# Layer 0's queries on four 64x64 quarters of TensorE, with a second copy of x by columns

## The chip, the core and the metric

The kernel runs on one core of one Trainium2 chip. A core has five engines that follow their own queues and meet by semaphores: TensorE (PE; its weight loads are listed apart as PEld), VectorE (DVE), ScalarE (ACT), GpSimd (POOL), and SyncE (SP), which here only issues DMAs. Matmuls write to PSUM, eight banks of 2 KB in each of 128 partitions. [...]The metric is the device time of one execution in microseconds.

## What is computed

Two graph layers over 16 batches of 1024 nodes with 64 features; `adj` is a 1024x1024 adjacency matrix for each batch, with some eight neighbours for a node and the node itself.

```python
# layer 0: eight heads of 64
q = (x @ Wq + bq);  k = (x @ Wk + bk);  v = (x @ Wv + bv)       # split in heads
s = leaky_relu(q k^T / 8 + edge_bias[adj], 0.2)                 # -1e9 where adj == 0
x = layernorm(x + (softmax(s) v) @ Wp + bp)
# layer 1: additive attention, one head
hp = x @ lin_w^T + lin_b;  u = hp W1^T;  v = hp W2^T
e = leaky_relu(u_i + v_j, 0.2) . a                              # masked by adj
x = layernorm(x + elu(softmax(e) hp))
```

Since few neighbours are set, the kernel builds a list of neighbours for every group of eight nodes and works on gathered columns alone. The weights of queries and keys are multiplied into one 64x64 matrix for each head beforehand (`aqk`), so that the scores of a node are its transformed x against its neighbours' plain x.

## The kernel before

**Tiles and steps.** A batch is eight tiles of 128 nodes. `xs` holds x with a row of the batch on each partition: partitions 0 to 63 have nodes of the first half of the batch (0 to 511), 64 to 127 of the second. Tile t is then 64 nodes of either half. `columns_T` turns it by matmuls against the identity into `xT`: partition d holds feature d of the first half, partition 64 + d feature d of the second, and columns `ts(t, 64)` are tile t's 64 nodes of each half.

One loop over steps g = 0, 1, ... does one tile of layer 0 and one of layer 1, which lags by 12 tiles, in a software pipeline whose order is written out by hand: a step gathers tile g, computes its queries, scores tile g-1, finishes tile g-2, and so on. Each engine gets its instructions in the order in which the program names them, so a queue's order is that of the loop's body. In the part that matters here a step issues:

1. `exps` and `score` of the tiles before (`s` L616, `sc` L624, `ls`, `mx`),
2. `gather` of layer 0's tile, both halves (`pg` L504, copied by ScalarE to `xg`, L510), with `heads` (`po` L684) between,
3. `rows` of layer 1 and, in odd steps, of layer 0 (`back`, L280 and L700),
4. `queries` (`pq` L599 on TensorE, `qp` L600 on VectorE),
5. the residuals (`o` L815, `y` L706 and the moments) and `den` L649 on VectorE,
6. layer 1's `project` (`pz` L750 and L756 on TensorE, Relu L761 on ScalarE, `r` L762 on VectorE),
7. layer 1's first gather half, its `turn_weights` (L790, copied as `eT` by VectorE, L792) and layer 0's `turn` (`pt` L523, copied as `xn` by ScalarE, L524),
8. `weigh` (`e` L776), which takes `r` and needs the bank that `eT` has read, the second gather half, `turn_weights` of layer 0 (`pp` L658, copied as `w`, L660), `attend` (`z` L668 and `pa` L801).

At five places of a step (`lists.place`) VectorE gets a share of the work that builds the next batch's neighbour lists; how much is due at each place is a fixed plan (`QUOTA`). At the end of step t == 4 of a batch, the next batch's `Layer0` is made: its constructor calls `begin`, which transposes x (`px` L274) and has ScalarE copy it to `xT` (L532). `score` of the next step is the next TensorE work.

**Banks.** PSUM's eight banks are shared by pools: `ps_g` (two banks: gathers, `pq`, `px`, layer 1's turn, `pa`), `ps_s` (two: scores, `pz`, `po`), `ps_p` (two: layer 0's turn `pt` and its turned weights `pp`), and `ps_z` (one each for two tags). A tile takes the bank that was used two tiles earlier in its pool and waits until that one's last reader is done.

**The queries.** For every head h and half n a matmul has 128 rows: `aqk[:, n, h, :]` holds the head's matrix on the 64 partitions of half n and zeros on the other 64, so the 128 rows of `xT` give half n alone. The outputs of the halves go to partitions `sub(n)`, 0 to 63 or 64 to 127, of one bank. A weight of 128 rows by 64 columns is shown as 128*64 in the profile; an fp32 matmul that is no transpose has two records.

Other parts of the kernel use all four quarters of TensorE, two blocks of 64 rows by two of 64 columns. They go through them in the order of `CORNERS`, with one bank for each row block:

```python
CORNERS = ((0, 0), (1, 1), (0, 1), (1, 0))      # (row block n, column block c_)
for n, c_ in CORNERS:                           # project, L756
    nc.tensor.matmul(pz[n][sub(c_), p, :], ub[sub(n), 2 * p + c_, :], rw[sub(n), :], start=False, stop=(p == 3))
```

`constants` (`prc` L585), `score` L616, `heads` L684 and `project` do so.

Of the kernel before, what the change touches and what calls it, by code (L numbers as in the profile page):

```python
# [9 lines left out]
F32 = mybir.dt.float32  # L10
I32 = mybir.dt.int32
AF = mybir.ActivationFunctionType
ALU = mybir.AluOpType
# [9 lines left out]
GR = 8  # L23
# [10 lines left out]
def kernel(  # L34
# [4 lines left out]
    nc = tc.nc  # L39
    B, N, D = x.shape  # L40
    H = edge_bias.shape[1]
    HD = H * D
    P = 128
# [9 lines left out]
    fst = fast.enter_context(tc.tile_pool(name="fst", bufs=1))  # L53
# [3 lines left out]
    ident = cst.tile([P, P], F32, name="ident")  # L57
# [7 lines left out]
    def sub(n):  # L65
        return slice(n * D, n * D + D)
# [6 lines left out]
    def bank(name):  # L73
        return ps_c.tile([P, 4, P], F32, tag="c", name=f"ps_{name}")

    def halves(name, cols_):

        t = fst.tile([P] + cols_, F32, tag=name, name=name)
        nc.gpsimd.memset(t, 0.0)
        return t  # L80
# [19 lines left out]

    bq_c, bk_c, bv_c = (columns(b, n) for b, n in ((bq, "bq_c"), (bk, "bk_c"), (bv, "bv_c")))
    QS1 = 1.0 / float(D) ** 0.5
    aqk = halves("aqk", [2, H, D])
    wvp = fst.tile([P, H, D], F32, name="wvp")
    qb = fst.tile([P, H], F32, name="qb")
    wc8 = halves("wc8", [GR, H, GR])
    wc1 = tmp.tile([1, H], F32, name="wc1")
    for h in range(H):
        c, r = h // 2, sub(h % 2)
        pw = bank(f"h_{h}")  # L110
        pc = bank(f"hc_{h}")
        for n in range(2):
            o = sub(n)
            nc.tensor.matmul(pw[o, 0, 0:D], wqT[r, c, :], wkT[r, c, :], start=True, stop=True)
            nc.tensor.matmul(pw[o, 1, 0:D], wvT[r, c, :], wp_l[r, c, :], start=True, stop=True)
            nc.tensor.matmul(pw[o, 2, 0:1], wkT[r, c, :], bq_c[r, c : c + 1], start=True, stop=True)
            nc.tensor.matmul(pw[o, 3, 0:1], wqT[r, c, :], bk_c[r, c : c + 1], start=True, stop=True)
            nc.vector.tensor_scalar(aqk[o, n, h, :], pw[o, 0, 0:D], QS1, None, ALU.mult)
            nc.vector.tensor_copy(wvp[o, h, :], pw[o, 1, 0:D])
            for i in range(GR):  # L120
                nc.vector.tensor_scalar(wc8[o, i, h, i : i + 1], pw[o, 3, 0:1], QS1, None, ALU.mult)
        nc.vector.tensor_scalar(qb[:, h : h + 1], pw[:, 2, 0:1], QS1, None, ALU.mult)
        nc.tensor.matmul(pc[0:1, 0, 0:1], bq_c[r, c : c + 1], bk_c[r, c : c + 1], start=True, stop=True)
        nc.vector.tensor_scalar(wc1[:, h : h + 1], pc[0:1, 0, 0:1], QS1, None, ALU.mult)
# [7 lines left out]
    pw = bank("wcb")  # L132
# [7 lines left out]
    pw = bank("bpv")  # L140
# [15 lines left out]
    pw = bank("ww")  # L156
# [7 lines left out]
    pw = bank("lin")  # L164
    for n in range(2):
        o = sub(n)
# [7 lines left out]
    pw = bank("ub")  # L174
# [5 lines left out]
    pw = bank("rows_b")  # L180
    nc.tensor.matmul(pw[:, 0, 0 : 2 * D], ones[0:1, :], ub_r.rearrange("o k d -> o (k d)"), start=True, stop=True)
    nc.vector.tensor_copy(rows_b.rearrange("p k d -> p (k d)"), pw[:, 0, 0 : 2 * D])
    NQ = D // GR
# [63 lines left out]
    CORNERS = ((0, 0), (1, 1), (0, 1), (1, 0))  # L247
# [12 lines left out]
    dbl = fast.enter_context(tc.tile_pool(name="g_dbl", bufs=2))  # L260
    sml = fast.enter_context(tc.tile_pool(name="g_sml", bufs=4))
    ps_g = fast.enter_context(tc.tile_pool(name="ps_g", bufs=2, space=bass.MemoryType.PSUM))
    ps_s = fast.enter_context(tc.tile_pool(name="ps_s0", bufs=2, space=bass.MemoryType.PSUM))
    ps_p = fast.enter_context(tc.tile_pool(name="ps_p", bufs=2, space=bass.MemoryType.PSUM))
# [2 lines left out]
    def by_rows(ap, n):  # L267
        return ap[n * 512 : n * 512 + 512, :].rearrange("(t r) d -> r t d", r=D)

    def columns_T(ps, src):  # L270

        for t in range(NT):
            for n in range(2):
                nc.tensor.matmul(ps[sub(n), ts(t, D)], src[:, t, :], ident[:, sub(n)], start=True, stop=True)  # L274

    def rows_T(ps, src, w):

# [184 lines left out]
    class Tiles:  # L462
# [63 lines left out]
        def begin(self, x_):  # L526

            b = self.b
            px = ps_g.tile([P, 512], F32, tag="g", name=f"px{self.layer}_{b}")
            columns_T(px, x_)  # L530
            self.xT = dbl.tile([P, 512], F32, tag=f"xT{self.layer}", bufs=2 - self.layer, name=f"xT{self.layer}_{b}")
            nc.scalar.copy(self.xT, px)  # L532
            self.t3, parts = thirds(x_, "x3", f"{self.layer}_{b}")
            self.f, self.xg, self.xn = {}, {}, {}
            lists.side.insert(0, parts)
# [5 lines left out]
    class Norm:  # L541


        def __init__(self, nm):
            self.nm = nm
            self.mv = sml.tile([P, NT, 2], F32, tag="mv", name=f"mv_{nm}")
# [20 lines left out]
    class Layer0(Tiles):  # L567
        layer = 0

        def __init__(self, b):  # L570
            self.b, self.cb, self.xs = b, {}, inputs[b]
            self.begin(self.xs)
            self.mx = dbl.tile([P, 2, NG // 4], F32, tag="mx", name=f"mx_{b}")
            self.y = dbl.tile([P, NT, D], F32, tag="y", bufs=3, name=f"y0_{b}")
            self.norm = Norm(f"0_{b}")
            self.qp, self.ls, self.den, self.w = {}, {}, {}, {}
# [16 lines left out]
        def queries(self, t):  # L593
            nm = f"{self.b}_{t}"
            qp = dbl.tile([P, NQ, H, GR], F32, tag="qp", name=f"qp_{nm}")
            pq = ps_g.tile([P, H, D], F32, tag="g", name=f"pq_{nm}")
            for h in range(H):
                for n in range(2):
                    nc.tensor.matmul(pq[sub(n), h, :], aqk[:, n, h, :], self.xT[:, ts(t, D)], start=True, stop=True)  # L599
            nc.vector.tensor_tensor(  # L600
                qp.rearrange("p q h i -> p h q i"), pq.rearrange("p h (q i) -> p h q i", i=GR),
                qb.unsqueeze(2).unsqueeze(3).to_broadcast([P, H, NQ, GR]), ALU.add,
            )
            self.qp[t] = qp

        def score(self, t, between):
# [274 lines left out]
    with tc.manual_schedule(engines={getattr(mybir.EngineType, e) for e in order}):  # L881
# [12 lines left out]
        for g in range(NT * B + LAG + 7):  # L894
            u = g - LAG
            b, t = divmod(g, NT)
# [472 lines left out]
```

## Time and profile before

| | |
|---|---|
| median of 3 runs | 2506.59 us (2506.02 to 2509.31) |
| the profiled execution | 2508.34 us, its span 2506.5 us |
| PE, PEld busy | 2296.7 us (92%), 1951.9 us (78%) |
| DVE, ACT, POOL busy | 1930.4, 1450.3, 1010.8 us |
| `pq` L599 | 4096 records, 222 ns each, 141.9 us busy |
| `qp` L600 | 128 instructions, 689 ns each, 88.2 us busy |
| `px` L274 of layer 0 | 512 records, 20.0 us busy |
| `xT` copy L532 | 32 instructions, 585 ns each |

Records of TensorE overlap, so 222 ns is the latency of one, not its share of the time; what a block costs is read from the starts in the timeline or from the chain. An engine's busy share is a mean over the span. The first 95 us are setup and the first batch's lists, the steps with queries run to 2344 us, and the rest is layer 1 alone.

### The profile page before, as it was taken

Reading aid. Unit: us, or ns where it says so; the run is one execution under the profiler, and the core shown is the slowest. Engines: PE = TensorE matmul, PEld = TensorE weight load, DVE = VectorE, ACT = ScalarE, POOL = GpSimd, SP = SyncE. Lnnn points to the kernel's source line nnn. Section 1 sums busy time; section 2 is a strip of 40 time slices with the busy share of each in tenths; the row PEclk is TensorE's granted clock in tenths of the full one; section 3 lists DMA queues with packets and bytes.
Section 4 is the critical chain, followed back from the end, with each engine's and each line's share of the span. In section 5 each row is a group of like instructions: output and inputs, shape, how many; then the busy total and the mean of one; then the engine's idle time right before and its main releaser. Section 6 shows DMA issues by size and latency. Waiting matters only on the chain.

```text
span 2506.5 us, 111153 instructions
## 1 busy us (share of the span) xinstructions
PE 2296.7 (92%) x48706; PEld 1951.9 (78%) x48706; DVE 1930.4 (77%) x5237; ACT 1450.3 (58%) x4401; POOL 1010.8 (40%) x1490
## 2 busy tenths in 40 slices
PE   5377999999999999999999999999999999999996
PEld 3266778888887888878888887878888887888864
DVE  6586868888887888888788878878787887866543
ACT  0054565666565665656566665656566665666743
POOL 1033433535344353534445353444534444443431
PEclk9988999999999999999999999999999999999998
DMA  3313242333224233323324232332423233231211
GB/s 102 109 43 117 81 143 77 104 116 109 91 81 138 77 117 103 121 77 100 120 77 140 81 119 77 113 107 78 142 86 113 83 111 103 66 96 61 69 38 29
DMA packets 192705, 239.03 MB, mean 95 GB/s; under 512 B 91732, under 2 KB 157332, under 8 KB 192212
## 3 DMA queue, kind: packets, MB, share of 16 engines
q1 hardware_dynamic: 192212, 231.85, 30.3%
q8 instruction: 384, 6.29, 1.0%
q14 instruction: 109, 0.89, 0.1%
HBM read 226.58 MB, written 5.21 MB: 92 GB/s over the span
## 4 chain that ended last, share of the span: by engine, by line
PE 66%; DVE 25%; DMA 3%; ACT 2%; issue 2%; POOL 1%; SPq 0%; POOLq 0%; ACTq 0%; DVEq 0%
PE pg L504 21%; PE s L616 5%; PE pt L523 5%; PE z L668 5%; DVE r L762 4%; PE pz L750 4%; PE pp L658 4%; PE pa L801 4%; PE pq L599 4%; PE pz L756 4%; PE po L684 3%; PE e L776 3%; DVE f L480 3%; DMA ad<-in_adj_dram 2%; PE pat L334 2%
## 5 line engine op out<-in xcount | busy, mean ns | idle before, releaser
L504 PE MATMUL pg<-f,x 128*64 128x272 bf16 (+2 forms) x13312 | 806.1, 273 | 40.4 <-DVE f L480 34.6
L504 PEld LDWEIGHTS <-x 128*64 128x64 bf16 x13312 | 662.8, 109 | 119.2 <-issue 73.8
L650 POOL TENSOR_TENSOR ls<-ls,den 128x480 f32<-128x480 f32 x256 | 298.5, 1166 | 579.8 <-DVE den L649 577.0
L510 ACT COPY xg<-pg 128x448 f32<-128x448 f32 x512 | 271.8, 531 | 392.4 <-PE pg L504 392.2
L480 DVE TENSOR_SCALAR f<-cb,jrow 128x2176 bf16<-128x2176 bf16 x512 | 409.0, 843 | 1.2 <-DMA cb<-col_d 1.0
L642 ACT ACTIVATE ls<-ls,mx 128x120 f32<-128x120 f32 x1024 | 391.2, 386 | 0.0
L524 ACT COPY xn<-pt 120x512 f32<-120x512 f32 x512 | 277.9, 598 | 22.7 <-PE pt L523 21.0
L523 PE MATMUL pt<-ident,xg 128*120 128x128 f32 x2048 | 269.6, 274 | 0.4
L761 ACT ACTIVATE r<-pz 128x480 f32<-128x480 f32 x256 | 132.2, 568 | 220.3 <-PE pz L756 220.3
L523 PEld LDWEIGHTS pt<-ident,xg 128*120 128x120 f32 x2048 | 229.4, 138 | 7.3 <-ACT xg L510 2.8
L489 POOL COPY xg<-xT 128x64 f32<-128x64 f32 x256 | 98.8, 396 | 307.1 <-PE pt L523 307.1
L762 DVE SCALAR_TENSOR_TENSOR r<-pz,r 128x480 f32<-128x480 f32 x256 | 155.9, 651 | 74.9 <-ACT r L761 74.6
L624 DVE TENSOR_TENSOR sc<-s,rowc 128x480 f32<-128x480 f32 x256 | 155.5, 649 | 71.2 <-PE s L616 69.3
L642 ACT ACTIVATION_READ_ACCUMULATOR ls<-ls,mx 128x1 f32 x1024 | 194.5, 190 | 0.0
L558 POOL TENSOR_TENSOR rs<-mv,eps 128x2 f32<-128x2 f32 x128 | 32.3, 253 | 379.0 <-DVE den L649 299.4
L632 DVE SCALAR_TENSOR_TENSOR ls<-sc 128x480 f32<-128x480 f32 x256 | 175.7, 686 | 0.0
L633 DVE TENSOR_REDUCE mx<-ls 128x4 f32<-128x480 f32 x256 | 167.2, 653 | 8.8
L756 PEld LDWEIGHTS pz<-rw,ub 64*64 64x64 f32 x4096 | 118.8, 133 | 63.2 <-issue 62.2
L600 DVE TENSOR_TENSOR qp<-pq,qb 128x512 f32<-128x512 f32 x128 | 88.2, 689 | 102.2 <-PE pq L599 101.0
L668 PE MATMUL z<-w,xn 120*64 120x64 f32 x4096 | 160.2, 229 | 4.8 <-ACT w L660 4.0
L658 PE MATMUL pp<-ident,ls 128*120 128x128 f32 x1024 | 143.0, 281 | 22.9 <-POOL ls L650 16.0
L668 PEld LDWEIGHTS z<-w,xn 120*64 120x64 f32 x4096 | 139.0, 141 | 28.6 <-ACT w L660 26.0
(212 smaller groups left out, 4092.7 us busy)
## 6 DMA issues: line engine op xcount, KB each, us to landing
cb<-col_d SPq DMA_DIRECT2D x271, 544.0 KB
ad<-in_adj_dram SPq DMA_DIRECT2D x256, 256.0 KB
xs<-in_x_dram SPq DMA_DIRECT2D x32, 128.0 KB
rows_s<-slot_d SPq DMA_DIRECT2D x256, 14.0 KB
out_dram<-o SPq DMA_DIRECT2D x32, 128.0 KB
col_d<-col SPq DMA_DIRECT2D x128, 4.2 KB
dg<-in_adj_dram SPq DMA_DIRECT2D x32, 2.0 KB
slot_d<-slot SPq DMA_DIRECT2D x16, 28.0 KB
```

The costliest lines, as they stand in the source:

```text
L480: nc.vector.tensor_scalar(fj.rearrange("p s n q k -> p (s n q k)"), cb.rearrange("p s n q k -> p (s n q k)"), jrow[:, j : j + 1], None, AL ...
L504: nc.tensor.matmul(pg[sub(n), :, FIRST * a_ + lo : FIRST * a_ + to], self.t3[:, k, 4 * hs + 2 * a_ + j, :], f[j][:, 2 * hs + a_, n, :, lo:to],
L510: nc.scalar.copy(dst, pg)
L523: nc.tensor.transpose(pt[:, q, :], xg[:, 4 * m + q, :], ident)
L524: nc.scalar.copy(self.xn[t][:, ts(m, 4), :], pt)
L632: nc.vector.scalar_tensor_tensor(ls, scs[n], SLOPE, scs[n], ALU.mult, ALU.max)
L642: nc.scalar.activation(ls[:, q, :], ls[:, q, :], AF.Exp, bias=neg[:, q : q + 1], accum_out=den[:, q : q + 1])
L650: nc.gpsimd.tensor_tensor(ls, ls, den.unsqueeze(2).to_broadcast([P, 4, SLOTS]), ALU.mult)
L658: nc.tensor.transpose(pt[:, p, :], ls[:, p, :], ident)
L668: nc.tensor.matmul(zz[sub(n), q, :], xn[:, q, sub(n)], w_[n][:, q // 2, sub(q % 2)], start=True, stop=True)
L756: nc.tensor.matmul(pz[n][sub(c_), p, :], ub[sub(n), 2 * p + c_, :], rw[sub(n), :], start=False, stop=(p == 3))
L762: nc.vector.scalar_tensor_tensor(r, pz[n], SLOPE / (1.0 - SLOPE), r, ALU.mult, ALU.add)
```

## The change

Before, `aqk` had for each half its own copy with zeros; now it is stored once on partitions 0 to 63 and once on 64 to 127, with no zeros, and a matmul uses 64 rows. Row block n computes heads 4n to 4n + 3, for both halves of the nodes. Row block 0 finds the first half of x in `xT`, but needs the second half on partitions 0 to 63 too, and row block 1 the first half on 64 to 127. So the constructor makes a second transpose `xo` with the halves exchanged (`columns_T` with `other=1`), again through a bank of `ps_g` and a ScalarE copy. The number of query matmuls stays 16 for a tile. Their outputs go to two banks, one for each row block, taken from `ps_p` and not from `ps_g`, and VectorE adds `qb` in two instructions of 256 columns, not one of 512.

```diff
-    aqk = halves("aqk", [2, H, D])
+    aqk = fst.tile([P, H, D], F32, name="aqk")
...
-            nc.vector.tensor_scalar(aqk[o, n, h, :], pw[o, 0, 0:D], QS1, None, ALU.mult)
+            nc.vector.tensor_scalar(aqk[o, h, :], pw[o, 0, 0:D], QS1, None, ALU.mult)
...
-    def columns_T(ps, src):
+    def columns_T(ps, src, other=0):
         for t in range(NT):
             for n in range(2):
-                nc.tensor.matmul(ps[sub(n), ts(t, D)], src[:, t, :], ident[:, sub(n)], start=True, stop=True)
+                nc.tensor.matmul(ps[sub(n), ts(t, D)], src[:, t, :], ident[:, sub(n ^ other)], start=True, stop=True)
...
             self.begin(self.xs)
+            px = ps_g.tile([P, 512], F32, tag="g", name=f"pxo_{b}")
+            columns_T(px, self.xs, 1)
+            self.xo = dbl.tile([P, 512], F32, tag="xo", name=f"xo_{b}")
+            nc.scalar.copy(self.xo, px)
...
-            pq = ps_g.tile([P, H, D], F32, tag="g", name=f"pq_{nm}")
-            for h in range(H):
-                for n in range(2):
-                    nc.tensor.matmul(pq[sub(n), h, :], aqk[:, n, h, :], self.xT[:, ts(t, D)], start=True, stop=True)
-            nc.vector.tensor_tensor(
-                qp.rearrange("p q h i -> p h q i"), pq.rearrange("p h (q i) -> p h q i", i=GR),
-                qb.unsqueeze(2).unsqueeze(3).to_broadcast([P, H, NQ, GR]), ALU.add,
-            )
+            pq = [ps_p.tile([P, H // 2, D], F32, tag="p", name=f"pq_{nm}_{n}") for n in range(2)]
+            for h in range(H // 2):
+                for n, c_ in CORNERS:
+                    src = self.xT if n == c_ else self.xo
+                    nc.tensor.matmul(
+                        pq[n][sub(c_), h, :], aqk[sub(n), H // 2 * n + h, :], src[sub(n), ts(t, D)], start=True, stop=True
+                    )
+            for n in range(2):
+                hs = slice(H // 2 * n, H // 2 * n + H // 2)
+                nc.vector.tensor_tensor(
+                    qp[:, :, hs, :].rearrange("p q h i -> p h q i"), pq[n].rearrange("p h (q i) -> p h q i", i=GR),
+                    qb[:, hs].unsqueeze(2).unsqueeze(3).to_broadcast([P, H // 2, NQ, GR]), ALU.add,
+                )
```

In the changed kernel the query matmuls are on L605; lines behind the constructor move by some ten.

## The prediction

> **What bounds the kernel now.** I read the chain of waits first, then the engine whose time it holds in the timeline, then the totals of who waited for whom. By engine the chain says:
>
> ```profile
> PE 66%; DVE 25%; DMA 3%; ACT 2%; issue 2%; POOL 1%; SPq 0%; POOLq 0%; ACTq 0%; DVEq 0%
> ```
>
> TensorE is the spine, and VectorE has a quarter. One step from the middle of the run shows how they meet (chain; columns are start, length, what):
>
> ```profile
> 1192.22 0.12 PE back L280 x4
> 1192.34 0.93 PE pq L599 x32
> 1193.27 0.96 PE pz L750 x8
> 1194.23 0.89 PE pz L756 x32
> 1195.13 0.56 ACT r L761
> ...
> 1195.71 1.22 DVE r L762 x2
> ...
> 1198.28 0.19 DVE eT L792
> ...
> 1198.51 0.67 PE e L776 x20
> ```
>
> The queries' block `pq` takes 0.93 us and everything up to `e` hangs on its end: the two `pz` blocks behind it on TensorE, the Relu on ScalarE, `r` and then `eT` on VectorE. The chain by line over the whole span gives `pq` 3.8%, that is 95 us; at 0.93 us each this is **102 of the 128 steps**. In the other 26 VectorE is late and the chain passes beside `pq`.
>
> The waits say the same (us in total, times, longest):
>
> ```profile
> DVE qp L600 <- PE pq L599: 101.0, 72, 4.8
> DVE r L762 <- ACT r L761: 74.6, 105, 2.1
> PE e L776 <- DVE eT L792: 73.2, 90, 1.9
> ```
>
> VectorE waits for `pq` in 72 steps, so a faster `pq` also starts its next operation earlier. Before `r` it waits for ScalarE in 105 steps, 0.71 us in the mean: there it has room. And TensorE waits for VectorE before `e`, so whatever delays `r` is paid in full.
>
> The rate of the blocks comes from the timeline of TensorE:
>
> ```profile
> 1202.52 1.14 PE L585 MATMUL prc<-xT,wc 64*64 64x32 f32 x64
> ...
> 1212.90 1.10 PE L599 MATMUL pq<-xT,aqk 128*64 128x64 f32 x32
> 1213.93 1.04 PE L750 MATMUL pz<-xg,w2d 64*64 64x480 f32 x8
> 1214.79 1.00 PE L756 MATMUL pz<-rw,ub 64*64 64x120 f32 x32
> ```
>
> A block lasts (n-1) intervals and one latency, the mean ns of its group. `pq`: (1.10 - 0.22) / 31 = 28.4 ns a record, 57 ns for each two. `prc`, on four quarters with 32 moving columns: (1.14 - 0.23) / 63 = 14.4 ns, 58 ns for each four. `pz` L756, four quarters, 120 columns: (1.00 - 0.26) / 31 = 23.9 ns, 95 ns for each four.
>
> **What the Trainium skill says.** "TensorEngine Tiling (Array Packing)", Available Configurations, has 128x64 as two tiles and 64x64 as four, and under Key Properties that tiles work in parallel: the trace agrees, 57 ns for two records of `pq` and 58 ns for four of `prc`. The same list says that a change of mode drains TensorE: the timeline has about 0.15 us from the last `pq` start (1212.90 + 0.88) to `pz` at 1213.93, against 0.03 us between records. "TensorE: Matmul & The Clock Gate", LDWEIGHTS, prices a weight load by columns alone, P/1.2: 53 ns for 64, whatever the rows, close to the 57 and 58 ns seen. "PSUM — Partial Sum Buffer", PSUM bank collisions, forbids two row tiles in one bank at once; that is why the new block has two banks. No run here shows that rule.
>
> **The change part by part.**
>
> 1. *The block itself.* 16 fp32 matmuls, 32 records, remain, but on four quarters. Two limits bound a group of four: the weight loads, 58 ns as in `prc`, and the moving data, 64 columns at 95/120 = 0.79 ns, 51 ns. The larger is 58, so 32 x 14.5 = 0.46 us in place of 0.93. The drain that stood behind `pq` now stands ahead of it; for an entry with cold weights I add 0.03 us: **0.49 us, a gain of 0.44**. No row shows 64 moving columns on four quarters, so the bounds are 0.46 us, and 0.67 us by a straight line between 14.4 ns at 32 columns and 23.9 at 120 taken up to 21 ns.
>    On the chain: 102 x 0.44 = **-44.9 us**. Where VectorE is late its `r` does not move and TensorE waits longer at `e`: 26 x 0. If all 128 counted at 0.46 it would be -59; if only 85 of them at 0.40, -34.
>
> 2. *The second transpose.* Once a batch, 16 matmuls against the identity and a ScalarE copy are added. The first one's block:
>
> ```profile
> 1154.62 0.98 PE px L274 x32
> 1155.60 1.19 PE s L616 x48
> ```
>
>    `s` follows at once, and in that step VectorE waits for TensorE, so nothing hides it: 15 x 0.95 = **+14.3 us** (32 records at 29 ns, a little over the `pq` cadence). The sixteenth, in the prologue, lies beside VectorE's lists and the DMA that the chain names until 94 us: 0. The copy (585 ns as L532) is next on ScalarE, ahead of the four exponentials of the next step; those stood 0.63 us behind the first transpose and now stand 0.63 us behind the second, so they move with TensorE: 0, and if they ended up late by a copy each time, 15 x 0.6 = +9. Bounds 7 (half hidden) and 23.
>
> 3. *VectorE's addition in two halves.* L600 takes 689 ns for 512 columns, L706 281 ns for 128, so 1.06 ns a column: 417 ns for 256. Two are 834, but one starts before the other ends (L624: two of 649 take 1.21-1.22 us in the timeline), so the end moves by 834 - 85 - 689 = 0.06 us. Where `pq` is on the chain, the room before `r` (0.24 us in the tightest steps that wait) covers it. In the 26 late steps it is paid: **+1.6 us**. Behind it on VectorE are `o`, `den`, then `r`, on which `e` waits; without cover it would be 128 x 0.06 = 7.7, with no overlap 128 x 0.145 = 18.6.
>
> 4. *Banks.* `pq` leaves the pool of the gathers for the two banks of the transposes L523 and L658. Its banks were last read by ScalarE's `w` of the step before, which `z` already waited for: 0. Layer 0's turn L523 must now find both halves of `qp` read. With layer 1 running, two `pz` blocks, a gather and L790 stand between, 3.4 us, against about 2.0 us plus 0.75 in the late steps: covered, and L790 waits for later VectorE work anyway. In the first 13 steps the turn follows directly and waits about 0.5 us; there `pp` waits for POOL still later, but where VectorE was 2 to 4 us late I put **+1 us** in all (bounds 0 and 6). The gathers lose a competitor: 0, bound -2.
>
> 5. *Setup.* One memset less on POOL, the same count on VectorE: 0, bound -1. SP's queue issues the same DMAs in the same order; the column lists and adjacency loads only come due sooner.
>
> Sum: -44.9 + 14.3 + 1.6 + 1.0 = **-28 us**. The profiled execution took 2508.3 us (span 2506.5), so its successor is put at 2480; it stood 1.7 us above the median of the runs, 2506.6, and from that I forecast **2479 us**.
>
> **The rivals.** *Half the rate:* 64 columns need 21 ns a record on four quarters, or ScalarE's extra copy delays the exponentials. For it: no row has this shape. Against: both limits that the rows show lie under it. 102 x 0.26 = -26.5, less 16.9, gives -10: 2497.
> *The quarters do not overlap* for this pattern, where neighbours take their moving data from two tiles, so `pq` stays at 28 ns: +16.9 us, **2523**, slower. It decides from 28.4 - 16.9 / 102 / 32 = 23 ns a record upwards. Against it: `prc`, `s` and `pz` use the same order of quarters and run below that, `prc` with two different slices of x.
> *VectorE becomes the bound:* if its room before `r` is gone in all steps, TensorE's gain ends as a longer wait before `e` and the two costs remain: +14.3 + 7.7, about 2529. Against it: 105 waits of 0.71 us; for it, the steps where `qp` starts late:
>
> ```profile
> 1270.54 0.60 DVE qp L600
> ...
> 1271.61 1.11 DVE r L762 x2
> ```
>
> *The change doesn't do what it says:* the order of instructions has 1,024 `pq` matmuls from each of the two copies of x and 256 more transposes, so this can be left out.
>
> **How the numbers follow.** As computed, 0.77 (own range 2466 to 2490, from 85 to 115 steps and 7 to 15 us for the transposes); half the rate 0.13; no overlap 0.05; VectorE 0.05. The range takes the first whole and most of the second: 2464 to 2498. A measurement of this kernel tells about 0.2%, 5 us, from no change. Faster by more: 0.77 and nearly all of the 0.13, 0.88; within it 0.03; slower 0.09.
>
> **What would show it.** In the profile after: L605 at about 14.5 ns a record, blocks of 0.5 us in the chain, some 2% of it; two `px` blocks in a row ahead of `s`, 1.9 us together; the addition as 256 instructions of about 420 ns; fewer waits of VectorE for `pq` in time, the wait before `e` longer only in the late steps; few waits of L523 on VectorE after the first 300 us. A cadence above 23 ns, or `r` no longer waiting for ScalarE, would prove it wrong.

## The result, and the profile after

| | before | after |
|---|---|---|
| median of 5 runs each | 2506.59 us (2505.05 to 2509.31) | 2495.43 us (2492.31 to 2497.38) |
| the profiled execution, its span | 2508.34, 2506.5 us | 2495.43, 2493.5 us |
| DVE busy, ACT busy | 1930.4, 1450.3 us | 1943.8, 1459.4 us |

The ratio is 0.9954, 95% interval 0.9943 to 0.9965: **faster, by 11.2 us in the medians** (13.0 by the spans), where 28 were forecast. 2495 lies inside the range, near its slow end, and beside the 2497 of the rival "half the rate". That rival did not come true, as the next lines show, so that the range held the result is in part luck.

The block itself came out as worked out. TensorE's timeline of the kernel after ("..." marks lines left out, here and below):

```profile
1207.23 0.27 PE L605 MATMUL pq<-xT,aqk 64*64 64x64 f32 x2
1207.24 0.27 PE L605 MATMUL pq<-xo,aqk 64*64 64x64 f32 x2
...
1207.70 0.22 PE L605 MATMUL pq<-xo,aqk 64*64 64x64 f32 x2
1207.74 0.99 PE L760 MATMUL pz<-xg,w2d 64*64 64x480 f32 x8
```

From the first to the last `pq` row are 0.47 us, where the block before took 0.88 (the starts of single records: 58.5 ns for each four). `pz` follows the last start by 0.04 us, where it stood 0.15 us off before. That pause has moved ahead of the block: from the last start of `back` to the first of `pq` are 152 ns in the median, 57 before. And the addition, from the page's groups (busy, mean ns | idle before):

```profile
L610 DVE TENSOR_TENSOR qp<-pq,qb 128x256 f32<-128x256 f32 x256 | 96.2, 418 | 78.9 <-PE pq L605 78.5
```

The chain by engine, and a stretch of it at the end of a tile 4:

```profile
PE 62%; DVE 30%; DMA 3%; issue 3%; ACT 1%; POOL 1%; SPq 0%; POOLq 0%; ACTq 0%; DVEq 0%
```

```profile
1147.78 0.98 PE px L274 x32
1148.76 0.93 PE pxo L274 x32
1149.69 1.19 PE s L626 x48
1150.89 1.75 PE pg L504 x29
1152.63 0.22 issue
...
1154.43 0.62 PE pq L605 x32
```

`pxo` stands on the chain with its full 0.93 us. TensorE's share of the chain fell from 66 to 62%, VectorE's rose from 25 to 30%, and 0.22 us of this stretch are "issue": TensorE stopped between two `pg` matmuls with no wait that the profile shows. The waits (us, times, longest):

```profile
PE e L786 <- DVE eT L802: 83.4, 89, 1.9
DVE qp L610 <- PE pq L605: 78.5, 75, 4.1
...
DVE r L772 <- ACT r L771: 53.2, 47, 2.1
...
DVE ab L325 <- DMA ad<-in_adj_dram: 32.6, 34, 2.4
...
PE pt L523 <- DVE qp L610: 15.2, 11, 4.5
```

`r` now waits for ScalarE in 47 steps and not in 105, the wait before `e` has grown by 10 us, and the turn L523 waits 15 us for `qp`.

**Where the time is, tile by tile.** I take the first `pq` start of every step and the time to the next one, after minus before: the median for the eight tiles of a batch, and the sum over steps 16 to 126 (14 batches, 13 for tile 7).

| tile | 0 | 1 | 2 | 3 | 4 | 5 | 6 | 7 |
|---|---|---|---|---|---|---|---|---|
| median, us | -0.25 | +0.03 | -0.25 | +0.07 | +0.89 | -0.47 | -0.47 | -0.17 |
| sum, us | -3.6 | +1.9 | -4.9 | -1.0 | +12.2 | -6.8 | -8.1 | -1.8 |

Tiles 5 and 6 have the full gain, 0.47 us a step. Tiles 1 and 3 are the late steps, in which `r` follows VectorE's own work without a pause. Missing against the forecast: about half the gain in tiles 0 and 2, two thirds in tile 7, 5 to 6 us in tile 4 beyond the transposes' 13, and some 3 us in the first 16 steps, counted from the start of the span (-0.7; sixteen of the 128 steps would have 3.5 of the 28).

**Tiles 0 and 2.** A step of tile 0 before and after, VectorE and POOL:

```profile
1071.39 1.22 DVE L762 SCALAR_TENSOR_TENSOR r<-pz,r 128x480 f32<-128x480 f32 x2 [0.24 <-ACT r L761]
...
1072.93 0.99 POOL L650 TENSOR_TENSOR ls<-ls,den 128x480 f32<-128x480 f32 x1
...
1073.39 0.56 DVE L431 TENSOR_SCALAR dgf<-dg 128x8 f32<-128x8 int32 x1
...
1074.35 0.28 DVE L792 COPY eT<-pt 120x128 f32<-120x128 f32 x1
```

```profile
1064.62 1.22 DVE L772 SCALAR_TENSOR_TENSOR r<-pz,r 128x480 f32<-128x480 f32 x2
...
1066.37 0.99 POOL L660 TENSOR_TENSOR ls<-ls,den 128x480 f32<-128x480 f32 x1
...
1066.61 0.78 DVE L431 TENSOR_SCALAR dgf<-dg 128x8 f32<-128x8 int32 x1
...
1067.79 0.28 DVE L802 COPY eT<-pt 120x128 f32<-120x128 f32 x1
```

L431 has eight columns and lasts 0.56 us, then 0.78: it ends with POOL's multiplication (1066.37 + 0.99 = 1067.36; 1066.61 + 0.78 = 1067.39), whenever it began. From `r` to `eT` are 2.96 us before and 3.17 after. L431 comes once a batch, in tile 0. In tile 2 another short instruction of VectorE's list stands at that place, L353, and it is held in the same way (before, after, and in e4 of the experiments below; its shortest, median and longest time in ns):

```profile
L353 DVE TENSOR_SCALAR flags<-lst x16: 160/554/607, 57.4 to 2126.0; 128x4 f32<-128x4 f32 x16
L353 DVE TENSOR_SCALAR flags<-lst x16: 158/775/778, 58.6 to 2116.7; 128x4 f32<-128x4 f32 x16
L353 DVE TENSOR_SCALAR flags<-lst x16: 158/159/606, 56.9 to 2088.7; 128x4 f32<-128x4 f32 x16
```

POOL starts that multiplication behind four operations of its own (L558 to L563), which follow VectorE's `o`, `y`, moments and `den`, which follow `qp`. So in these steps `eT`, and `e` behind it, hang on VectorE's list and not on TensorE's `pz`. Counted from the first `pq` start, medians of tiles 0 and 2, `r` starts 0.56 us sooner than before, `qp` only 0.41 (the pause ahead of `pz` was not in its way) and `den`, behind two additions for one, 0.34; `eT` comes 0.34 sooner, with `den`. "SBUF — State Buffer", Who interferes with whom, in the Trainium skill says that a `tensor_scalar` in a two-port mode and GpSimd take a shared pair of ports for a whole instruction, and that the other blocks fully; the trace agrees with a block to the end of POOL's instruction. That the ports are what holds it no run here shows.

### The profile page after: what moved, and what is told of

Same layout as the page of the kernel before. It is cut to its first block, busy times and chain, and to the rows that moved or that the text cites. A ratio compares the mean times of both kernels' runs of the same rounds, so it can differ in the third digit from the quotient of the medians.

```text
span 2493.5 us, 112320 instructions
## 1 busy us (share of the span) xinstructions
PE 2260.5 (91%) x49218; PEld 1910.4 (77%) x49218; DVE 1943.8 (78%) x5365; ACT 1459.4 (59%) x4417; POOL 1017.8 (41%) x1489
## 3 DMA queue, kind: packets, MB, share of 16 engines
q8 instruction: 388, 6.36, 1.0%
## 4 chain that ended last, share of the span: by engine, by line
PE 62%; DVE 30%; DMA 3%; issue 3%; ACT 1%; POOL 1%; SPq 0%; POOLq 0%; ACTq 0%; DVEq 0%
PE pg L504 20%; PE pt L523 5%; PE s L626 5%; DVE r L772 4%; PE z L678 4%; PE pp L668 4%; PE pa L811 4%; PE po L694 3%; DMA ad<-in_adj_dram 3%; DVE f L480 3%; PE e L786 3%; PE pq L605 3%; DVE qp L610 2%; PE pat L334 2%; PE pz L766 2%
## 5 line engine op out<-in xcount | busy, mean ns | idle before, releaser
L523 PE MATMUL pt<-ident,xg 128*120 128x128 f32 x2048 | 271.6, 275 | 15.7 <-DVE qp L610 15.2
L523 PEld LDWEIGHTS pt<-ident,xg 128*120 128x120 f32 x2048 | 230.7, 138 | 23.7 <-DVE qp L610 16.7
L489 POOL COPY xg<-xT 128x64 f32<-128x64 f32 x256 | 107.9, 432 | 291.3 <-PE pt L523 291.3
L558 POOL TENSOR_TENSOR rs<-mv,eps 128x2 f32<-128x2 f32 x128 | 32.3, 253 | 359.2 <-DVE den L659 280.6
L610 DVE TENSOR_TENSOR qp<-pq,qb 128x256 f32<-128x256 f32 x256 | 96.2, 418 | 78.9 <-PE pq L605 78.5
L748 POOL TENSOR_TENSOR ub<-u,in_q 128x512 f32<-128x512 f32 x128 | 155.4, 1215 | 0.1
```

Source lines behind the costliest of these rows:

```text
L523: nc.tensor.transpose(pt[:, q, :], xg[:, 4 * m + q, :], ident)
```

## The experiments

All are timed in five rounds against the kernel before (median 2508.63 us beside the first four, 2507.52 beside the next four, 2505.52 beside the last two); "us under before" is against that median. In the table, tile columns are the medians of the tile table above, for that kernel's trace, which is one execution. From 310 to 2330 us the granted clock is 1.00 in every trace, so that these columns compare like with like; from 99 to 310 us, where the first 16 steps lie, it is 0.89 before and 0.87 to 0.94 in the others.

| kernel | median us | ratio to before, 95% | us under before | tile 0 | 1 | 2 | 4 | 7 |
|---|---|---|---|---|---|---|---|---|
| the change | 2495.43 | 0.9954 (0.9943, 0.9965) | 11.2 | -0.25 | +0.03 | -0.25 | +0.89 | -0.17 |
| e1_px_alone | 2526.15 | 1.0071 (1.0057, 1.0086) | -17.5 | 0.00 | +0.21 | -0.01 | +1.18 | +0.15 |
| e2_no_px | 2468.77 | 0.9849 (0.9831, 0.9868) | 39.9 | -0.25 | -0.16 | -0.26 | -0.47 | -0.47 |
| e3_xo_dma | 2478.17 | 0.9875 (0.9856, 0.9895) | 30.5 | -0.25 | -0.10 | -0.25 | -0.47 | -0.44 |
| e4_divide_first | 2461.81 | 0.9818 (0.9798, 0.9839) | 46.8 | -0.86 | +0.11 | -0.87 | +1.07 | -0.28 |
| e5_ad6 | 2470.31 | 0.9844 (0.9826, 0.9862) | 37.2 | -0.24 | -0.27 | -0.24 | +0.67 | -0.08 |
| e6_dma_divide | 2448.37 | 0.9762 (0.9744, 0.9780) | 59.2 | -0.86 | -0.08 | -0.86 | -0.47 | -0.47 |
| e7_before_divide | 2488.83 | 0.9919 (0.9901, 0.9937) | 18.7 | -0.39 | 0.00 | -0.39 | 0.00 | 0.00 |
| e8_half_add | 2473.74 | 0.9864 (0.9846, 0.9883) | 33.8 | -0.57 | -0.11 | -0.57 | +0.47 | -0.47 |
| e9_dma_divide_ad6 | 2428.47 | 0.9701 (0.9684, 0.9718) | 77.1 | -0.86 | -0.43 | -0.86 | -0.47 | -0.47 |
| e10_px_later | 2486.55 | 0.9927 (0.9913, 0.9940) | 19.0 | -0.24 | -0.11 | -0.25 | -0.47 | -0.38 |

### The second transpose

**e1_px_alone**: the kernel before, with the transpose and its copy added and nothing reading them (`columns_T` gets its `other` as in the change).

```diff
             self.begin(self.xs)
+            px = ps_g.tile([P, 512], F32, tag="g", name=f"pxo_{b}")
+            columns_T(px, self.xs, 1)
+            self.xo = dbl.tile([P, 512], F32, tag="xo", name=f"xo_{b}")
+            nc.scalar.copy(self.xo, px)
```

> The kernel before with the second transpose and its ScalarE copy alone; the queries don't read them. Theory: the transpose lies on the path in 14 or 15 batches at 0.93 us (the trace after has 0.933 us from px to s more in every batch), so +13 to +14 us; if the added instructions also bring the waits of TensorE for its own instructions that the trace after has (15 us of such stops in the steady part against 9 before), up to +20. Rival: the copy delays the exponentials on ScalarE, +20 to +30. Rival: hidden, under +4.

17.5 us slower. Tile 4's sum is +18.5: some 13 are the transposes, the rest lies with stops of TensorE. I count as a stop a start of a matmul, within a block, at least 0.2 us later than usual for its line while no semaphore holds it. In tile 4, between 300 and 2340 us, there are none before, seven here (6.0 us) and eight in the kernel after (6.0 us). In all twelve traces 189 of the 194 stops end 1.2 to 1.6 us after a packet of the instruction queue has landed; of the whole time, some 7% lies so behind a packet.

**e2_no_px**: the changed kernel without the transpose; all query matmuls read `xT`, so that half of them take the wrong half of x.

```diff
-            px = ps_g.tile([P, 512], F32, tag="g", name=f"pxo_{b}")
-            columns_T(px, self.xs, 1)
-            self.xo = dbl.tile([P, 512], F32, tag="xo", name=f"xo_{b}")
-            nc.scalar.copy(self.xo, px)
...
-                    src = self.xT if n == c_ else self.xo
+                    src = self.xT
```

> The changed kernel without the second transpose and its copy: all query matmuls take their moving data from xT, so that half of the queries use the wrong half of x. Against the kernel before. Theory: 11.2 us gained by the change plus 13 to 14 for the transpose, so -24 to -25 us (2482); if the additional stops for instructions come from the transpose too, -30 (2476). If instead the shortfall against the forecast is all in the transpose's side effects, -42.

39.9 us under before, 28.7 more than the change has. Tile 4 accounts for 18.4 us of that by its sum, tile 1 for 4.7, tile 7 for 4.8, the first 16 steps for 4.4. So the transposes cost the changed kernel twice their own length. Tiles 0 and 2 stay at -0.25: something else holds them.

**e3_xo_dma**: the same halves brought to `xo` by DMA.

```diff
-            px = ps_g.tile([P, 512], F32, tag="g", name=f"pxo_{b}")
-            columns_T(px, self.xs, 1)
             self.xo = dbl.tile([P, 512], F32, tag="xo", name=f"xo_{b}")
-            nc.scalar.copy(self.xo, px)
+            for n in range(2):
+                nc.sync.dma_start(self.xo[sub(n), :], self.xT[sub(1 - n), :])
```

> The changed kernel with xo made by two DMAs from xT (the halves of the partitions exchanged) in place of 16 matmuls and a copy. Queries of that batch come four steps later, so a landing of a few us is hidden. Theory: as without the transpose, 2482 (2476 if the stops for instructions go too). Rival: the DMA's wait for xT stands in SP's queue ahead of adjacency loads and delays them: 2490 to 2495.

30.5 us under before, 19.3 more than the change has; by the medians, tiles 4 and 7 have their gain back. No query waits for the two transfers. Tile 4 has two stops left (1.4 us), but the trace as a whole has 21 (16.1 us), about as many as after: others came in tiles 2 and 3 (five, 5.2 us). So it is tile 4 that is relieved, and not TensorE's stops in sum.

**e10_px_later**: the second transpose and its copy, taken out of the constructor into a method of their own, `other`, at the end of tile 5's step (for the first batch right behind the constructor).

```diff
             if t == 4 and b + 1 < B:
                 l0[b + 1] = Layer0(b + 1)
+            if t == 5 and b + 1 < B:
+                l0[b + 1].other()
```

> The changed kernel with the second transpose of x issued one step later: at the end of the step of tile 5, the first one staying at the end of tile 4's. Same work, same instruction count; no two transposes in a row. It asks why tile 4 lost 6.8 us to stops of TensorE, on top of the transposes' own 13. Theory that the stops come from two blocks of small matmuls in a row, which use up the instructions faster than they are brought: tile 4 falls from +0.89 to about -0.45 us against the kernel before, tile 5 rises from -0.47 to about +0.46, and the stops of tile 4 largely vanish: 5 to 8 us faster than the changed kernel, ratio to the kernel before about 0.992 to 0.9935. Rival: the stops fall where the packets happen to end, so as many come elsewhere: the same time within 2 us, ratio 0.995. Second rival: the ScalarE copy, now ahead of tile 6's exponentials, is on the path: 0.996 or more.

19.0 us under before, 7.8 more than the change has. The chain at the ends of tiles 4 and 5:

```profile
1146.18 0.98 PE px L274 x32
1147.16 1.19 PE s L629 x48
1148.36 2.91 PE pg L504 x47
...
1162.47 0.98 PE pxo L274 x32
1163.45 1.19 PE s L629 x48
```

Tile 4 is at -0.47 and tile 5 at +0.51, which is -0.47 and one transpose of 0.98: the sum over both tiles falls from +5.4 to +1.1 us. Stops between 300 and 2340 us fall from 22 (14.2 us) to 12 (5.3 us), in tile 4 from eight to two. So **tile 4's stops come with the two transposes in a row**, and are not the transposes' own time. "Runtime: NRT & Kernel Launch", Instruction fetch mechanics, says that instructions are fetched in blocks of 16 KiB on an own queue and that this is mostly hidden. The packets of that queue are 16 KB here (6.36 MB in 388), and if the fetch is what stops TensorE, it was not hidden behind the two transposes: in the kernel after, a stop follows them within 6 us in eight batches. The number of records in a row can't be all: `prc` has 64 too, at 14 ns each, and in the same trace a stop follows within 8 us of only two of its blocks. That the fetch is the cause is argued from the timing of the packets; no run changed the fetch itself.

### VectorE and POOL

**e4_divide_first**: the changed kernel with the first share of `divide` (`den` and, on POOL, `ls`) ahead of the residuals.

```diff
+            at(l0, g - 2, "divide", 1)
             at(l1, u - 3, "residual")
             at(l0, g - 3, "residual")
-            at(l0, g - 2, "divide", 1)
```

> The changed kernel with the reciprocal and POOL's multiplication of the second half (divide 1) named ahead of the residuals. In tiles 0 and 2 of a batch the trace after has VectorE's L431 end just when POOL's L660 ends, 0.78 us in place of 0.56, and eT there moves 0.34 us where r moved 0.56. Theory: VectorE is held by POOL's operation; with POOL's operation 1 us earlier L431 is short, two steps a batch gain about 0.2 us: -4 to -8 us against the changed kernel (2488 to 2491). Rival: VectorE's own queue sets eT there, or POOL's other operations hold it in the same way: no change, 2495; or slower if the residual is then late.

46.8 us under before, 35.6 more than the change has (27.4 by the spans; the profiled execution took 6 us more than the median): the direction as expected, the size four times or more. Its step of tile 0:

```profile
1044.77 0.99 POOL L660 TENSOR_TENSOR ls<-ls,den 128x480 f32<-128x480 f32 x1 [3.28 <-DVE rs L824]
...
1046.08 1.22 DVE L772 SCALAR_TENSOR_TENSOR r<-pz,r 128x480 f32<-128x480 f32 x2
...
1048.07 0.16 DVE L431 TENSOR_SCALAR dgf<-dg 128x8 f32<-128x8 int32 x1
...
1048.63 0.28 DVE L802 COPY eT<-pt 120x128 f32<-120x128 f32 x1
```

POOL multiplies before `r` begins, L431 takes 0.16 us, and from `r` to `eT` are 2.55 us, 0.62 less than after. I had expected only the part that the change had added to the block, 0.22 us, to go; the whole went, in tiles 0 and 2 (16.5 us by the sums). The first 16 steps gave 12 more, at a granted clock of 0.92 for 0.89.

**e7_before_divide**: the same edit in the kernel before.

> The kernel before with divide 1 ahead of the residuals, nothing else. In it L431 takes 0.56 us where 0.16 is its length without POOL in the way. Theory: 0.40 us in two steps of 14 batches, 11 us, and some 9 us in the first steps, where TensorE waits for POOL: -20 us (2487). Rival: the hold costs nothing there because r came later in the kernel before, -9 or less; then the hold is a new wait that the change made.

18.7 us under before (15.8 by the spans): tiles 0 and 2 at -0.39, 11.3 us in sum, the other medians at zero. **The block was there before, 0.40 us of it, and the change lengthened it by 0.22.** The 9 us expected in the first steps did not come (1.2), so that the total is near the expected 20 by luck. With the block gone in both kernels, the change is worth 46.8 - 18.7 = 28 us (24.6 by the spans). That this is the forecast's number is chance: it is a different sum, with the stops still in it and a larger gain in the first steps.

**e8_half_add**: ScalarE copies the second half of `qp`, which then lacks `qb`, and VectorE adds to the first half alone.

```diff
+            hs = slice(H // 2, H)
+            nc.scalar.copy(qp[:, :, hs, :].rearrange("p q h i -> p h q i"), pq[1].rearrange("p h (q i) -> p h q i", i=GR))
-            for n in range(2):
+            for n in range(1):
```

> The changed kernel with the second half of qp copied by ScalarE without qb (left out for heads 4 to 7), so that VectorE has one of the two additions. Theory: VectorE is on the path in four of eight tiles (0 to 3): it gains up to 0.33 us in tiles 1 and 3, where it is late, and 0.2 us in tiles 0 and 2, where den and POOL's operation start earlier: -12 to -16 us against the changed kernel (2480 to 2484). Rival: the addition's length doesn't matter where other work of VectorE comes before it, or ScalarE's copy delays the Relu: 2493 to 2500.

33.8 us under before, 22.6 more than the change has, where 12 to 16 were expected. Tiles 0 and 2 gain another 0.32 each and tile 3 0.33: in tiles 0, 2 and 3, and a little in tile 1, VectorE's addition lies on the path; in tile 5 it doesn't (-0.47 as before). Tile 4 gains as well, in a trace with fewer stops (16 for 22); tile 7 does so in its median but not in its sum (-1.1 for -1.8).

### The adjacency loads

**e5_ad6**: the changed kernel with six adjacency tiles in flight, not four.

```diff
-                ads[k] = dbl.tile([P, 2, SEG], I32, tag="ad", bufs=4, name=f"ad_{b}_{hs}_{T}")
+                ads[k] = dbl.tile([P, 2, SEG], I32, tag="ad", bufs=6, name=f"ad_{b}_{hs}_{T}")
...
-        for k in range(4):
+        for k in range(6):
...
-                load(hs * NT + T + 4)
+                load(hs * NT + T + 6)
```

> The changed kernel with six buffers and six loads ahead for the adjacency tiles in place of four. In the trace after VectorE waits 32.6 us for these loads (27.3 before, 24.6 without the second transpose), and in tile 7 TensorE stops 0.33 us ahead of L334 where it did not before. Theory: these waits are on the path in part, -3 to -8 us against the changed kernel (2487 to 2492). Rival: the loads only stand in the queue longer, no change within 2 us.

37.2 us under before, 26 more than the change has, far beyond what I expected. The wait for the loads, from the waits of this kernel:

```profile
DVE ab L325 <- DMA ad<-in_adj_dram: 4.9, 5, 1.5
```

It was 32.6 us after and 27.3 before, so the change had added only 5. The first 16 steps give 14 us here, 3.7 of them ahead of the first step, and tile 1's sum falls from +1.9 to -8.0. By these waits the kernel before had this loss nearly in full, so that it is hardly a missing part of the change; no run gave the kernel before six tiles.

### Put together

**e6_dma_divide**: e3's and e4's edits.

> The changed kernel with both: xo by two DMAs, and divide 1 ahead of the residuals. If the two gains add (0.9954 - 0.9875 and 0.9954 - 0.9818 of the kernel before), the ratio is 0.974, about -65 us. If they share a cause, it stays near that of divide alone, 0.98.

59.2 us under before, 48.0 more than the change has: most of the 54.9 that e3 (19.3) and e4 (35.6) gave singly.

**e9_dma_divide_ad6**: e5's edit added.

> The changed kernel with three edits together: xo by two SP DMAs from xT in place of the second transpose, the first share of divide's work ahead of the residuals, and six adjacency buffers loaded six tiles ahead. The three took about 19, 34 and 25 us off the changed kernel alone or nearly so (ratios to the kernel before 0.9875, 0.9818, 0.9844, against 0.9954), and the first two together stand at 0.9762. Theory: the adjacency wait is a separate loss of VectorE, mostly in the first steps and in tile 1, so the third still adds 10 to 25 us: ratio 0.966 to 0.972, about 2425 to 2438 us. Rival: the first steps can only be gained once, since the earlier divide already took 11 us there, and the rest of that wait is hidden by TensorE: 0.973 to 0.977, no gain over the two. By tile, theory has tile 1 about 0.3 us shorter than with the two edits.

The theory's 0.966 to 0.972 held: 0.9701, **77.1 us under before**, the best here. Tile 1 is 0.35 us shorter than in e6, and the first 16 steps give 15.9 us.

**The first 16 steps and the clock.** What they gain in a run goes roughly with the clock that was granted from 99 to 310 us: 1 to 2 us lost in e3 and e10 (0.88, 0.87), 3.0 gained in e8 (0.88), 0.7 after (0.89), 5.0 in e2 (0.91), 7.9 and 12.8 in e6 and e4 (0.92), 14.5 in e5 (0.93), 23.9 in e9 (0.94). By an estimate from these figures the clock is at most 11 us of e9's gain, 211 us x (0.94 - 0.89). Whether it gave the time or came of fewer waits no run separates, so what the edits are worth in these steps is not shown.

## Why the prediction was wrong in its size

**Step 1, the block.** Right: 58.5 ns for four records (58 forecast), and from the last start ahead of the block to `r` are 0.47 us less (0.44). **What failed is the count, 102 x 0.44.** That `pq` lies on the chain in 102 steps says that the first nanosecond saved there counts, not that all 440 do. In tiles 0 and 2 a second path, through VectorE's list and POOL to the short instruction that POOL holds (L431, L353), ended 0.22 us behind the first; in sum these tiles gave 8.5 us where 28 steps of 0.47 are 13.2.

**Step 2, the transposes.** Their own time was right (0.93 us behind `px` and 0.98 alone, for 0.95), the term was not: tile 4 lost 6 us to stops beside them, e10 showed that these go when the blocks are apart. I had bounded the sum from above with 23 us for a copy that comes late; the copy was free, and the stops took its place. By e2 the transposes cost 28.7 us in all, beyond that bound too, of which 4.4 are in the first steps.

**Step 3, the addition.** The sizes were right (418 ns each, two in 0.76 us by the timeline for the 0.75 worked out). That the room before `r` covers it was the false sentence. `r` did start early enough: in e8, where it has 0.35 us of room again, it starts at the same 2.98 us after the first `pq` in tiles 0, 2 and 4. But the hold by POOL behind it did not move with it. e8 shows the addition on the path in tiles 0, 2 and 3, so "VectorE becomes the bound" was half true.

**Step 4, the banks.** L523 waits 15.2 us in the first 300 us where I put 1 on the clock; the wait of `pp` for POOL fell from 16.0 to 8.2 us meanwhile, so that about half of it is not new waiting in sum. That the first 16 steps gained 0.7 and not 3.5 us fits with it, but no run took this wait away alone.

**Step 5** and the copy at nothing held, as far as the table can tell.

By sums over steps 16 to 126, against a full gain of 0.47: 4.7 us are missing in tiles 0 and 2, 5.5 in tile 4 and 4.3 in tile 7, while tiles 5 and 6 gave some 2 more than that; with 3 in the first steps this is about the 15 us between 28 and 13.

**Open:** tile 7. Its stops grew from 2.8 to 5.7 us (four to nine), which is most of the 4.3 that it lacks. In e3 they are 4.5 us; the median there (-0.44) hides them, since they fall in few batches, but in sum the tile has 3.4 of its 6.1. Why they came in tile 7 is not shown. Open too is why tile 1 improves when the transposes are gone or apart, and what the first steps, which e2 improved and e3 and e10 did not, owe to the clock.

## What to carry to other kernels

A part of the chain that gets shorter gains only down to the next path. Before multiplying a saving by the steps in which it lies on the chain, ask of the instruction where the paths meet how late its *other* inputs and its engine were, and look there for short instructions with long durations: one of 160 ns that lasts 560 is a wait that no view lists as one. And where blocks of short matmuls are put in a row, look for stops behind them too; here they cost tile 4 6.0 us beside the 13 of the matmuls themselves.

## What the runs showed of the hardware

Two VectorE operations of eight and four columns (L431, int32 to float, and L353) took about 160 ns where POOL's multiplication was out of the way (medians of e4). Beside it they took medians of 558 and 554 ns before, 778 and 775 after, and ended within 30 ns of it in 13 of their 16 times. Not every POOL operation held them: L353, begun beside L559 of two columns, took 158 ns in the kernel after.

TensorE's stops of 0.2 to 1.6 us, 9 us between 300 and 2340 us before and 14 after, all end 1.2 to 1.6 us after a 16 KB instruction packet lands. In tile 4 there were none before and eight after, where 64 records of 29 ns stand in a row.

Four quarters with 64 moving columns keep the cadence of 32 columns, 58 ns a group. A pause of about 0.1 us beyond the usual lies where the shape of the quarters changes (152 ns from start to start); the change moved it and did not remove it.
